# Attention in a fused attention pair: fp32 for a fourth of the first image's keys, earlier first scores, and two changes of order

## The chip, the cores and the metric

The kernel runs on one core of a Trainium2 chip. The metric is the device time of one execution in microseconds. Before the change the median of three runs is 2675.47 us (2675.39 to 2676.53). In what follows PE is TensorE (matmuls), DVE is VectorE, ACT is ScalarE, POOL is GpSimd, and SP is the engine that issues most of the transfers.

## The reference, cut to what matters

Two layers stand one after the other. Each has a group norm, attention over the 1024 positions of an image, a projection and a residual addition. The first layer has 8 heads of 64 channels, and its q, k and v go through an 8-bit quantization whose scale is taken over all 8 images. The second has one head of 512 channels.

```python
# layer 0: x is (8, 512, 32, 32), T = 1024, 8 heads
h = group_norm(xf, gn_w, gn_b)
qkv = jnp.einsum('oc,bct->bot', qkv_w, h) + qkv_b[None, :, None]
q, k, v = jnp.split(qkv.reshape(b * NUM_HEADS, -1, T), 3, axis=1)
q = fake_quant(q); k = fake_quant(k); v = fake_quant(v)
w = jnp.einsum('bct,bcs->bts', q * scale, k * scale)
w = jax.nn.softmax(w.astype(jnp.float32), axis=-1).astype(q.dtype)
a = jnp.einsum('bts,bcs->bct', w, v)
x = xf + jnp.einsum('oc,bct->bot', proj_w, a) + proj_b[None, :, None]
# layer 1: one head of 512
t = group_norm(x).transpose
qk = jnp.einsum('bnd,bmd->bnm', q, k) * scale
out = jnp.einsum('bnm,bmd->bnd', jax.nn.softmax(qk, axis=-1), v)
x = x + out @ wp.T + bp
```

## The kernel before, in words

**Three stages.** The first (0 to about 612 us) makes q, k and v of all eight images and stores them in DRAM, since the quantization needs the extremes of all of them. The second (612 to about 773 us) runs image 0's attention, and beside it `fold`: the second layer's weights are multiplied with one another, in eight pieces of four fp32 matmuls (`fold`, four into `wa` and four into `wm`), followed by two weighings of biases (`wt_f`, `wc_f`). In the third, `layer1(b)` of image b fills PE while the attention of image b + 1 is laid in between.

**Attention (`attention`, L832).** A unit is one pair of heads, one half `hf` of 512 queries and one block `s` of 128 keys; an image has 4 pairs x 2 halves x 8 blocks = 64 units. `scores` (L844) makes the scores in a PSUM pair `st`, of which there are two (two matmuls, one per head of the pair), and ACT writes their exponentials to `pt` (fp32, four buffers). `split` (L867) turns `pt` into two fp16 parts: a cast to fp16 gives the first, and a subtraction on DVE, pt minus the first part, gives the second. The cast stands on POOL for s = 2 and 6, on DVE for s = 1 and 5 as long as the order is not planned, and on ACT otherwise. `over_keys` (L897) sums v over the keys with both parts (four matmuls of 64 output columns into `av`), `totals` (L913) sums ones over them (four matmuls of 32 columns into `sm`). After a half, `finish` copies `av` to `ao` and `sm` to `rs` on ACT; after the second half the row sums go through DRAM, are inverted, and `ao` is scaled.

**The order.** The generator yields after every four units. In each such advance the scores of units u + 6 and u + 7 come first, then the sums of u and u + 1, the scores of u + 8 and u + 9, and the sums of u + 2 and u + 3 (`dense`), or all four units' sums at once (not `dense`). During `fold` an `advance()` runs whenever `pos < (folded - F_FIRST) * A_IMAGE / F_FOLD`; with F_FIRST = 12 the first scores stand after the fourth piece. Two advances more (`LEAD`) follow image 0, on image 1's units, and then the order of DVE, ACT and PE is written out: `InOrder` gives each instruction a dependency on the one before, and `later` puts chores with a cost and a due time into a list from which `fill` takes them; `settle(name)` issues all chores of a name at once.

**Loads.** `load_pair` (L795) fetches q, k and v of a pair into `raw` buffers (two), and two DVE steps each (`quant`, `quant2`) quantize them. With two buffers, v's load waits until q's has been read.

**Layer 1.** `o_run` (L1277) makes the second layer's attention output in seven products (`seven`), whose sums of operands are made by DVE: p2 for the third product, p3 for the fourth, p4 later. At its first product it yields 1, which lets an advance of attention in, and only then settles p2. In `first` (L1486), the next image's projection yields -1 between its halves (a dense advance) and 1 after the second. Projection and scores share the PSUM pool `ps_s`.

Of the kernel before, what the change touches and what calls it, by code (L numbers as in the profile page):

```python
# [9 lines left out]
F32 = mybir.dt.float32  # L10
# [7 lines left out]
P = 128  # L18
B, C, HH, WW = 8, 512, 32, 32
T = HH * WW  # L20
# [33 lines left out]
def attn_pair_kernel(  # L54
# [12 lines left out]
    class InOrder:  # L67
# [71 lines left out]
        def settle(self, what):  # L139

            while True:
                i = next((i for i, c in enumerate(self.chores) if c[0] == what), None)
                if i is None:
                    return
                self.begin(i)
# [143 lines left out]
    with ExitStack() as fast:  # L289
# [4 lines left out]
        def av_bank(name):  # L294
            return ps_v.tile([P, 512], F32, tag="v", name=name)
# [480 lines left out]
        def inverse(sm, rows, at, scratch, nm):  # L776
# [13 lines left out]

            return rest

        ao = {}

        def load_pair(b, j):  # L795

            nm = f"{b}_{j}"
            raws = []

            def fetch(i, src):  # L800
                raw = raw_p.tile([P, T], F32, tag="raw", name=f"raw_{nm}_{i}")
                nc.sync.dma_start(
                    raw if i < 2 else raw.rearrange("p (t d) -> p t d", t=NT), src
                )
                raws.append(raw)

            fetch(0, q_d[b][j])
            fetch(1, k_d[b][j])
            qt = qkp.tile([P, T], BF, tag="q", name=f"q_{nm}")
            kt = qkp.tile([P, T], BF, tag="k", name=f"k_{nm}")  # L810
            vt = qkp.tile([P, NT, P], F16, tag="v", name=f"v_{nm}")
            todo = (qt, kt, vt.rearrange("p t d -> p (t d)"))

            def quants(i):
                for step in (quant, quant2):
                    dve.later(
                        "qk" if i < 2 else "qv", 0.7, lambda step=step: step(raws[i], todo[i], i),
                        pe.t + 12.0, 45.0,
                    )

            def fetch_v():
                fetch(2, v_d[b][:, :, bass.ts(j, P)])
                quants(2)

            quants(0)
            quants(1)
            dve.later("qk", 0.0, fetch_v)
            return qt, kt, vt

        settle = dve.settle  # L830

        def attention():  # L832
# [8 lines left out]
            pts, parts, avs, sms, rss, ready = {}, {}, {}, {}, {}, {}  # L841
            st_free, at_hand = [0.0, 0.0], set()

            def scores(u):  # L844
                b, j, hf, s = units[u]
                if hf == 0 and s == 0:
                    settle("qk")
                nm = f"{b}_{j}_{hf}"
                qt, kt, _ = pairs[b, j]
                st = pair_ps(f"st_{nm}_{s}")  # L850
                awaits(st_free[-2])
                for i, r in enumerate(HALF):
                    mm(
                        st[:, i, :], lhsT=kt[r, bass.ts(s, P)],
                        rhs=qt[r, bass.ts(hf, 512)], start=True, stop=True,
                    )
                if u >= 4:
                    need(u - 4)
                pt = ptp.tile([P, 2, 512], F32, tag="p", name=f"pt_{nm}_{s}")
                there = act.do(  # L860
                    1.12, lambda: act.activation(pt, st, AF.Exp, scale=esc),
                    max(pe.t + 0.25, ready.get(u - 4, 0.0) + 0.1),
                )
                st_free.append(there)
                pts[u] = pt, there

            def split(u):  # L867

                b, j, hf, s = units[u]
                pt, there = pts.pop(u)  # L870
                two = partp.tile([P, 2, 2, 512], F16, tag="two", name=f"two_{b}_{j}_{hf}_{s}")
                parts[u] = two

                def rest():
                    dve.tensor_tensor(two[:, 1], pt, two[:, 0], ALU.subtract)
                    ready[u] = dve.t

                def cast(copy=act.copy):
                    at_hand.add(u)
                    copy(two[:, 0], pt)  # L880
                    done_at = act.t if copy == act.copy else there + 1.5
                    dve.later("sum", elements(1024), rest, done_at + 0.1, 9.0)

                if s % 4 == 2:
                    cast(nc.gpsimd.tensor_copy)
                elif not InOrder.planned and s % 4 == 1:
                    cast(dve.tensor_copy)
                else:
                    act.later("cast", 1.02, cast, there, 7.0)
# [7 lines left out]
            def over_keys(us):  # L897
                need(us[-1])
                awaits(ready[us[-1]])
                pe.t += 0.12  # L900
                for u in us:
                    b, j, hf, s = units[u]
                    if s == 0:
                        avs[b, j, hf] = av_bank(f"av_{b}_{j}_{hf}")
                    for w in range(2):
                        for i, r in enumerate(HALF):
                            mm(
                                avs[b, j, hf][r, :], lhsT=pairs[b, j][2][:, s, r],
                                rhs=parts[u][:, w, i, :], start=(s == 0 and w == 0),
                                stop=(s == NT - 1 and w == 1),  # L910
                            )

            def totals(us):  # L913
                pe.t += 0.12
                for u in us:
                    b, j, hf, s = units[u]
                    if s == 0:
                        sms[b, j, hf] = av_bank(f"sm_{b}_{j}_{hf}")
                    two = parts.pop(u)
                    for n in range(4):  # L920
                        mm(
                            sms[b, j, hf][n * QUAD : (n + 1) * QUAD, :], lhsT=ones16,
                            rhs=two[:, n // 2, n % 2, :], start=(s == 0), stop=(s == NT - 1),
                        )

            def finish(b, j, hf):

# [43 lines left out]
            for u in range(0, len(units), 4):  # L971
                b, j, hf, s = units[u]
                if hf == 0 and s == 0:
                    n = b * PAIRS + j + 1
                    if n < B * PAIRS:
                        pairs[divmod(n, PAIRS)] = load_pair(*divmod(n, PAIRS))
                    settle("qv")

                def two(what, v):
                    if v < len(units):
                        what(v)
                        what(v + 1)

                pe.t += 0.12
                two(scores, u + 6)
                if dense:
                    over_keys((u, u + 1))  # L990
                    totals((u, u + 1))
                    two(split, u + 6)
                    two(scores, u + 8)
                    over_keys((u + 2, u + 3))
                    totals((u + 2, u + 3))
                else:
                    over_keys(range(u, u + 4))
                    totals(range(u, u + 4))
                    two(split, u + 6)
                    two(scores, u + 8)  # L1000
                if s == NT - 4:
                    finish(b, j, hf)
                two(split, u + 8)
                pe.t += 0.15
                last = (j, hf, s) == (PAIRS - 1, NH - 1, NT - 4)
                yield 6.0 + (hf == NH - 1 and s == NT - 4), b + last
# [270 lines left out]
        def o_run(b, hf, vt, vs, ps_, pts, acc, rx, between):  # L1277
# [50 lines left out]
            for step in seven(  # L1328
# [2 lines left out]
                lambda n, ps: act.do(0.59, lambda: act.copy(u[n], ps)), whole, add,  # L1331
            ):
                if step == 1:
                    yield 1
                elif step == 2:
                    settle("p2")
                elif step == 3:
                    settle("p3")
                if step == 2 + (hf == NH - 1 and not final):
# [47 lines left out]
        def layer1(b, steps):  # L1387
# [36 lines left out]
            for hf in range(NH):  # L1424
# [39 lines left out]
                def third(p12=p12, p22=p22):  # L1464
# [2 lines left out]

                dve.later(
                    "p2", elements(1024), lambda t1=t1, t2=t2, p22=p22: tt(t2, p22, t1, ALU.subtract),
                    dve.t, 5.0,  # L1470
                )
                dve.later("p3", elements(1024), third, act.t, 9.0)
                dve.later(
# [10 lines left out]
                if b + 1 < B and last:  # L1484

                    def first():  # L1486
                        nonlocal ahead
                        yield -1
                        yield from project(b + 1, score_bank)
                        yield 1  # L1490
                        ahead = norm1(b + 1, score_bank)
                        next(ahead)

                    def more():
                        next(ahead)
                        yield from ()

                    between = [first, more, more]
# [93 lines left out]
        att = attention()  # L1592
        A_IMAGE = PAIRS * (NH * NT * 1.5 + 1.0)
        F_FOLD = 4.0 * 8 + 2.0
        F_FIRST = 12.0
        pos, done = 0.0, 0
        dense = True

        def advance():
            nonlocal pos, done  # L1600
# [26 lines left out]
            e.t = pe.t  # L1627
        InOrder.planned = True
        for n in others():
            dense = n < 0  # L1630
            advance()


# [362 lines left out]
```

## Time and profile before

| what | us |
|---|---|
| median of three runs | 2675.47 |
| the profiled execution | 2674.34 |
| its span, first to last instruction | 2672.5 |
| PE busy in it | 2582.6 (97%) |
| DVE, ACT, POOL busy | 1909.5, 1263.1, 204.1 |
| PE waiting between 612 and 775 us for exponentials (`pt`) | 30.7 |
| first scores of image 0 | 626.83 |
| first projection matmul of image 0 | 773.58 |

The busy times are sums over the whole span, and the stages differ: in the first and third PE hardly waits, in the second it does. So a row is read by its stage. A row of waits names the engine and what it would have gone on with, then the engine whose work ended last among what it waited for. Rows in order of time give start, length, engine, operation, output and inputs; an instruction's length can overlap with the next one's by a tenth of a microsecond, so that the spacing of a run of equal ones is shorter than the length of one.

### The profile page before, as it was taken

The page shows a single profiled execution, that of the slowest core. Times are in us where ns is not written, and L with a number is a line of the kernel's source. Part 1 is how long each engine was busy: PE and PEld are TensorE (multiplying, and loading weights), DVE is VectorE, ACT ScalarE, POOL GpSimd, SP SyncE. Part 2 cuts the span into 40 slices and gives each one's busy share as a digit, 9 for nine tenths or more (in the row PEclk, how much of TensorE's full clock was granted, in tenths as well). Part 3 has the DMA queues.
Part 4 walks back from the last instruction along what each step waited for, and adds up shares of the span by engine and source line. Part 5 has one row for each costly group of instructions (what it writes and reads, how often), then busy time and mean ns, then how long its engine had stood idle before and what let it go on. Part 6 is the DMA issues. An engine that isn't in the chain of part 4 may idle for free.

```text
span 2672.5 us, 33466 instructions
## 1 busy us (share of the span) xinstructions
PE 2582.6 (97%) x13150; PEld 1663.0 (62%) x13150; DVE 1909.5 (71%) x2755; ACT 1263.1 (47%) x1588; POOL 204.1 (8%) x157
## 2 busy tenths in 40 slices
PE   8999999998788999999999999999999999999998
PEld 4655555553225775776577567757765775677687
DVE  7866666558987767886777677768867776876544
ACT  0111111115866674666566556646664665564121
POOL 0000000001220000000100010001001000100000
PEclk9999999999899999999999999999999999999999
DMA  5233232134321132223212321322132123212211
GB/s 201 112 125 126 110 119 94 73 124 150 121 67 45 57 108 83 84 68 102 96 60 76 111 88 56 107 84 84 58 109 99 60 76 107 86 42 73 106 36 37
DMA packets 146888, 241.97 MB, mean 91 GB/s; under 512 B 26528, under 2 KB 92064, under 8 KB 145184
## 3 DMA queue, kind: packets, MB, share of 16 engines
q1 hardware_dynamic: 115872, 181.50, 20.3%
q10 hardware_dynamic: 30848, 58.23, 6.4%
q8 instruction: 105, 1.72, 0.3%
q14 instruction: 63, 0.52, 0.1%
HBM read 152.86 MB, written 86.28 MB: 89 GB/s over the span
## 4 chain that ended last, share of the span: by engine, by line
PE 80%; DVE 8%; issue 7%; ACT 2%; DMA 1%; POOL 1%; ACTq 0%; SPq 0%; DVEq 0%; POOLq 0%
PE s L201 15%; PE o L201 14%; PE qkps L201 10%; PE pj L201 8%; PE av L201 7%; PE v2ps L201 7%; PE g L201 6%; PE vps L201 5%; PE st L201 4%; PE sm L201 4%; DVE two L86 2%; ACT pt L86 1%; DVE sums L86 1%; DVE x L86 1%; DVE h L86 1%
## 5 line engine op out<-in xcount | busy, mean ns | idle before, releaser
L86 DVE TENSOR_TENSOR two<-pt,two 128x1024 f16<-128x1024 f32 x512 | 618.4, 1225 | 164.7 <-POOL two L880 131.1
L86 ACT ACTIVATE pt<-st,esc 128x1024 f32<-128x1024 f32 x512 | 543.8, 1114 | 371.4 <-PE st L201 349.9
L86 ACT CAST two<-pt 128x1024 f16<-128x1024 f32 x364 | 369.3, 1054 | 9.6 <-issue 5.6
L880 POOL CAST two<-pt 128x1024 f16<-128x1024 f32 x128 | 179.5, 1402 | 1578.7 <-PE sm L201 1352.0
L86 ACT ACTIVATE u<-qkps,qkb 128x512 f32<-128x512 f32 x90 | 61.8, 687 | 500.8 <-PE qkps L201 500.8
L201 PE MATMUL av<-two,v 128*64 128x512 f16 x2048 | 254.3, 386 | 0.6
L201 PE MATMUL s<-g,h 128*128 128x256 f32 x1024 | 234.1, 381 | 0.0
L201 PE MATMUL pj<-ao,wp 128*128 128x512 f32 x512 | 223.9, 595 | 1.1 <-DVE ao L86 1.1
L201 PEld LDWEIGHTS s<-g,h 128*128 128x128 f32 x1024 | 193.0, 190 | 31.7 <-issue 4.3
L201 PE MATMUL st<-q,k 64*128 64x512 bf16 x1024 | 166.6, 387 | 40.0 <-ACT pt L86 33.5
L201 PEld LDWEIGHTS <-v 128*64 128x64 f16 x2048 | 103.8, 110 | 132.7 <-issue 61.4
L201 PE MATMUL s<-g,sums 128*128 128x256 f32 x768 | 178.4, 381 | 0.2 <-DVE p L86 0.2
L201 PE MATMUL o<-p,v 128*128 128x256 f32 x768 | 175.2, 382 | 0.0
L201 PEld LDWEIGHTS pj<-ao,wp 128*128 128x128 f32 x512 | 96.1, 190 | 122.6 <-issue 112.6
L201 PE MATMUL qkps<-sums,wa 128*128 128x512 f32 x360 | 164.9, 592 | 0.1
L201 PEld LDWEIGHTS o<-p,v 128*128 128x128 f32 x768 | 144.4, 190 | 25.6 <-issue 6.9
L201 PEld LDWEIGHTS s<-g,sums 128*128 128x128 f32 x768 | 144.8, 190 | 24.1 <-issue 4.5
L201 PE MATMUL sm<-two,ones 128*32 128x512 f16 x2048 | 141.8, 386 | 1.9 <-ACT rs L86 1.9
L201 PE MATMUL qkps<-x,wqkv 128*128 128x512 f32 x304 | 140.8, 602 | 1.3 <-DVE x L86 1.3
L201 PEld LDWEIGHTS <-k 64*128 64x128 bf16 x1024 | 36.4, 94 | 163.9 <-issue 161.9
L201 PE MATMUL o<-g,vsum 128*128 128x256 f32 x512 | 123.7, 397 | 11.5 <-DVE g L86 11.5
L201 PE MATMUL g<-h,wa 128*128 128x256 f32 x512 | 120.6, 384 | 1.7 <-DVE h L86 1.7
(193 smaller groups left out, 3524.9 us busy)
## 6 DMA issues: line engine op xcount, KB each, us to landing
rs<-rs_d SPq DMA_DIRECT2D x80, 256.0 KB
x<-in_x_dram SPq DMA_DIRECT2D x32, 512.0 KB
raw<-q_d SPq DMA_DIRECT2D x32, 512.0 KB
raw<-k_d SPq DMA_DIRECT2D x32, 512.0 KB
v_d<-v SPq DMA_DIRECT2D x32, 512.0 KB
raw<-v_d SPq DMA_DIRECT2D x32, 512.0 KB
x_d<-h SPq DMA_DIRECT2D x64, 256.0 KB
x<-x_d ACTq DMA_DIRECT2D x64, 256.0 KB
```

The lines of the kernel that those rows point to most:

```text
L86: ins = self.latest = op(*args, **kw).ins
L201: ins = nc.tensor.matmul(ps, lhsT=lhsT, rhs=rhs, **kw).ins
L880: copy(two[:, 0], pt)
```

## The change

Image 0's units with s = 3 and s = 7 (`plain`) are no longer split: their exponentials go into a buffer `aside` of three slots, and `over_keys` and `totals` take them as fp32, with an fp32 copy of v's blocks 3 and 7 (`vfs`, made by a third DVE step `whole`) and the fp32 ones. The cast on DVE stays for s = 5 alone. The first v has a buffer of its own (`raw_first`, one of the `ao` buffers), and its load is issued at once. F_FIRST goes from 12 to 4. In `o_run`, p2 is settled before the yield of the first product, and its chore's due time is set to be first. After the second half of a projection, `first` yields 2, for which the advance has another order (`late`): sums of u and u + 1, scores of u + 6, totals, sums and totals of u + 2 and u + 3, then splits and scores of u + 8.

```diff
+        def plain(b, s):
+            return b == 0 and s % 4 == 3
...
             def fetch(i, src):
-                raw = raw_p.tile([P, T], F32, tag="raw", name=f"raw_{nm}_{i}")
+                if (b, j, i) == (0, 0, 2):
+                    raw = aop.tile([P, NH, 512], F32, tag="ao", name="raw_first").rearrange(
+                        "p h n -> p (h n)"
+                    )
+                else:
+                    raw = raw_p.tile([P, T], F32, tag="raw", name=f"raw_{nm}_{i}")
...
+            def whole(raw, _, i):
+                quant2(raw.rearrange("p (t d) -> p t d", t=NT)[:, 3::4, :], vfs[j], i)
...
+            if b == 0:
+                vfs[j] = xp.tile([P, 2, 256], F32, tag="x", name=f"vf_{nm}")[:, :, 0:P]
...
-                for step in (quant, quant2):
+                for step in (quant, quant2, *([whole] if i == 2 and b == 0 else [])):
...
             def fetch_v():
+                if len(raws) == 2:
+                    fetch(2, v_d[b][:, :, bass.ts(j, P)])
+                quants(2)
+
+            if (b, j) == (0, 0):
                 fetch(2, v_d[b][:, :, bass.ts(j, P)])
-                quants(2)
-
...
+            aside = l2p.tile([P, 3, NT // 2, 256], F32, tag="vsum", name="aside")
...
-                pt = ptp.tile([P, 2, 512], F32, tag="p", name=f"pt_{nm}_{s}")
+                if plain(b, s):
+                    pt = aside[:, u // 4 % 3].rearrange("p (i k) n -> p i (k n)", i=2)
+                else:
+                    pt = ptp.tile([P, 2, 512], F32, tag="p", name=f"pt_{nm}_{s}")
...
+                if plain(b, s):
+                    parts[u], ready[u] = pt, there
+                    return
...
-                elif not InOrder.planned and s % 4 == 1:
+                elif not InOrder.planned and s == 5:
...
+                    if plain(b, s):
+                        for i, r in enumerate(HALF):
+                            mm(
+                                avs[b, j, hf][r, :], lhsT=vfs[j][:, s // 4, r],
+                                rhs=parts[u][:, i, :], start=False, stop=(s == NT - 1),
+                            )
+                        continue
...
+                    for n in range(2 if plain(b, s) else 4):
+                        row = sms[b, j, hf][n * QUAD : (n + 1) * QUAD, :]
+                        if plain(b, s):
+                            mm(row, lhsT=ones[:, 0:QUAD], rhs=two[:, n, :], start=False,
+                               stop=(s == NT - 1))
+                        else:
+                            mm(row, lhsT=ones16, rhs=two[:, n // 2, n % 2, :], start=(s == 0),
+                               stop=(s == NT - 1 - (b == 0 and n > 1)))
...
-                two(scores, u + 6)
-                if dense:
+                if not late:
+                    two(scores, u + 6)
+                if late:
+                    over_keys((u, u + 1))
+                    two(scores, u + 6)
+                    totals((u, u + 1))
+                    over_keys((u + 2, u + 3))
+                    totals((u + 2, u + 3))
+                    two(split, u + 6)
+                    two(scores, u + 8)
+                elif dense:
...
                 if step == 1:
+                    settle("p2")
                     yield 1
-                elif step == 2:
-                    settle("p2")
...
                     "p2", elements(1024), lambda t1=t1, t2=t2, p22=p22: tt(t2, p22, t1, ALU.subtract),
-                    dve.t, 5.0,
+                    0.0, 0.5,
...
                         yield from project(b + 1, score_bank)
-                        yield 1
+                        yield 2
...
-        F_FIRST = 12.0
+        F_FIRST = 4.0
...
-            dense = n < 0
+            dense, late = n < 0, n == 2
```

More of the change, by code (lines that the diff above doesn't have):

```diff
@@ L791, in inverse @@
             return rest
+        vfs = {}
+        def plain(b, s):
+            return b == 0 and s % 4 == 3
         ao = {}
@@ L919, in totals @@
                     two = parts.pop(u)
[L920 to L924, printed above, removed]
+                    for n in range(2 if plain(b, s) else 4):
[6 more added lines that the diff above has]
+                               stop=(s == NT - 1 - (b == 0 and n > 1)))
             def finish(b, j, hf):
@@ L1594, in attn_pair_kernel @@
         F_FOLD = 4.0 * 8 + 2.0
-        F_FIRST = 12.0
+        F_FIRST = 4.0
         pos, done = 0.0, 0
         dense = True
+        late = False
         def advance():
```

## The prediction

> **What bounds the kernel now.** I read the page's chain first, then TensorE's waits over the whole span, then the same waits by stretch, then the order of time at the two places where they pile up. All times are of the one profiled execution. The chain's shares by engine, and the waits (total, times, longest):
>
> ```profile
> PE 80%; DVE 8%; issue 7%; ACT 2%; DMA 1%; POOL 1%; ACTq 0%; SPq 0%; DVEq 0%; POOLq 0%
> ```
>
> ```profile
> PE st L201 <- ACT pt L86: 33.5, 50, 1.6
> PE o L201 <- DVE g L86: 11.5, 6, 1.9
> ...
> PE st L201 <- DVE h L86: 6.2, 12, 0.5
> ```
>
> TensorE sets the end, and is busy 97%, so a gain has to come out of its few waits or its busy time. These three waits hold 51 us. By stretch, 30.7 of the 33.5 us for `pt` fall between 612 and 775 us, where image 0's attention runs with only the folding beside it; the other two recur in the later images: six times 1.9 us before an `o` product, and twelve times 0.52 us before scores that follow a half of the projection.
>
> ```profile
> 720.00:760.00 40.00, 29.11 (x226) 8.80 (x223) 39.06 (x39) 35.99 (x39) 12.99 (x6) 0.87 0.25 80
> ```
>
> This is a row of the busy times by stretch: length, then PE, its weight loads, DVE, ACT, POOL, then granted clock and DMA. In image 0's attention DVE (39.06 of 40) and ACT (35.99) are full and PE is not. How this stage starts:
>
> ```profile
> 621.81 6.53 DMA raw<-v_d
> ```
>
> ```profile
> 633.09 6.07 PE L201 MATMUL fold<-wn_v 128*128 128x512 f32 x8
> ...
> 645.47 3.70 PE L201 MATMUL fold<-wn_v 128*128 128x512 f32 x8
> ```
>
> The first line is of the chain followed back from 660 us: it runs over the load of the first v, which waits for q's raw buffer. The other two are of the order of time: the folding piece at 633 took 6.07 us, the same piece at 645 3.70.
>
> ```profile
> 991.79 0.25 DVE L86 RECIPROCAL rcs<-rcs 128x16 f32<-128x16 f32 x1
> ...
> 994.36 1.23 DVE L86 TENSOR_TENSOR two<-pt,two 128x1024 f16<-128x1024 f32 x1 [2.31 <-ACT two L86]
> ...
> 1002.79 1.22 DVE L86 TENSOR_TENSOR g<-p,g 128x1024 f32<-128x1024 f32 x1
> ...
> 1004.06 3.72 PE L201 MATMUL o<-g,vsum 128*128 128x256 f32 x16 [1.91 <-DVE g L86]
> ```
>
> The sum `g<-p,g` (p2 in the code) has had its data since 991.78, when the exponential of p ends, but stands on DVE behind a burst of attention's subtractions, while DVE idles 2.31 us at 992.
>
> [...] the four 32-wide `wt_f` products (8 records, two of 0.43 us for each matmul) take 1.03 to 1.06 us together. [...] The piece of 6.07 us agrees; it follows 6 us of sparse scores with a granted clock of 0.61 in 630 to 635. [...] The casts on POOL agree: 1.04 us alone, up to 3.55 beside DVE.
>
> **Part A, image 0 in fp32 for a fourth of the keys.** For 16 of 64 units the cast and the subtraction go, and s = 1 is cast on ACT where DVE did it. Spacings from back-to-back rows: exponential 1.01, ACT cast 0.95, copy 0.47, DVE subtraction 1.13, DVE cast 0.60, quantizing step 0.68.
> Per half (8 units), before: ACT 8 x 1.01 + 4 x 0.95 + 2 x 0.47 = 12.8; DVE 8 x 1.13 + 2 x 0.60 + 3 x 0.68 + 0.75 = 13.05. Copies of `ao` mark the ends of the halves: 654.80, 670.35, 685.61, 700.58, 717.87, 732.94, 747.72, 761.34, 775.06; the two clean ones take 13.62 and 13.72, 0.6 over DVE's sum.
> After: ACT 8.08 + 3 x 0.95 + 0.94 = 11.9; DVE 6 x 1.13 + 0.60 + 3 x 0.68 + 0.25 + 0.75 = 10.4. ACT becomes the bound. PE: a split unit costs 0.25 (scores) + 0.49 + 0.27; in a plain one av is 0.86 and sm 0.86, if the two halves run together. No row shows a 64-wide fp32 pair; from below 0.86 by `wt_f`, from above 1.72 in series. I take 0.86: 6 x 1.01 + 2 x 1.97 = 10.0 per half. In order: counted from the start of the first exponential of a group, PE has given out that group's second scores at 0.5, does 0.49 + 0.86 + 0.27 + 0.86 = 2.5 us of sums with a plain unit, and the next scores by 3.45, where ACT is busy until 2 x 1.01 + 2 x 0.95 = 3.9: it fits, by 0.45. Clean half: 11.9 + 0.5 = 12.4.
> With a folding piece (3.44 + a copy of 0.58 on ACT, both ahead of the next exponential) that cover is gone: scores come at 3.0 + 3.45 + 0.5, and ACT waits about 3.2. Half: 11.9 + 3.2 + 0.4 = 15.5, no better than now (15.55, 15.26, 14.97).
>
> **Part B, earlier start.** F_FIRST = 4 puts the first scores after two pieces (PE 619.8, q and k quantized at 619.85) instead of four (626.83). v's own buffer waits for a PE read that ends at 610, so its load is issued about 610.2, ahead of q_d and k_d stores on SP, which are due at 611.0 anyway; against 6.53 us for the same load later it lands about 616, before its place on DVE at 617.8. If late, q and k stand behind it: up to 1 us. The fp32 copy of v waits for those stores, about 622.5 to 624.5; behind it stand the z sums and the first subtraction, due about 627, needed by exponential 5 at 627.8. Counted at nothing, up to 1.4 if not. Pair 1's q and k, behind the 1 MB of `wp` on SP but no longer behind v, land by about 630, before their place. The buffers taken (one `ao` of five, `vsum`, two of `x`) are next wanted after 764, when they are free: nothing.
> The two pieces come back into the attention, so it meets six, not four. Going through the order by hand (exponential 0 at 620.6, 1.01 each, casts 0.95, the next piece at half clock like the one at 633, so 6.1), the first half's `ao` copy is at 647.5 instead of 654.80: 7.3.
> Then four halves with a piece 4 x 15.5, one with the weighing of biases 16.3 (its stall of 3.5 on ACT by the same chain, and 0.5 for the last `wc_f`), two clean 2 x 12.4, and image 1's first half, which is split throughout and has now five ACT casts: 14.3. Sum 117.4 against 120.3: 2.9. Stage: 7.3 + 2.9 = 10.2 us, from 4 to 15.
>
> **Part C, the sum ahead of the burst.** p2 moves into the idle 2.31 us at 992, takes 1.2, delays nothing. The `o` product then starts at 1002.15. Late next: the third operand. DVE after the kept_u addition: three acc at 0.69 from 1002.79, then the 1.13 us sum, done at 1006.07; PE needs it at 1005.80 + 0.36 = 1006.16. It fits by 0.1. 6 x 1.91 = 11.5, at least 9. For the other half of each image (seen at 907.87) DVE now waits 1.7 us for the exponential with three subtractions behind it; the one that is needed, for PE's fourth pair of av at about 910.9, ends at 908.65. Nothing.
>
> **Part D, late order.** After the second half of a projection the av of two units (0.98 us) now stand before the scores, and cover DVE's eviction (0.52). The scores, and so the exponentials, start about 1 us later, with PE filled till 1052.6 when the eighth needs its slot at 1051.75. I take 0.4 x 6 = 2.4 us, from 0 to 3.1. The first half of each projection keeps its wait.
>
> **Sum.** 10.2 + 11.5 + 2.4 = 24.1. The profiled execution took 2674.34 (span 2672.5 and 1.84 around it), 1.1 below the median of the runs, 2675.47: 2650.2 on it, 2651.3 on the median. I say 2651.
>
> **Rivals.**
> The stage gives nothing, the waits do: the 64-wide pairs run in series (0.86 more for av, so 1.3 per half over the cover, about 10 in all). For: no such row; against: `wt_f`. 2661.
> The next wait takes p2's place: one subtraction more ahead of the third operand costs 6 x 1.1 = 6.6, 2658. For: cover of 0.1 only; against: the order in the program puts none there.
> The pieces cost ACT less, as now, where a half with one is about 1.5 over a clean one: five times about 1.7 less, 2642. For: those halves; against: PE has 2 us more in each now.
> Slower: in the plain units each 64- or 32-wide fp32 product runs alone with its two weight loads (0.11 each) in the open: 4 x 1.08 = 4.3 us per unit for 1.72, 2.6 more; 16 x 2.6 less the cover of 16 x 0.25 is 38, so 2689. It decides from 24.1 / 16 + 0.25, 1.8 us per unit. Against: loads of f16 weights lie under the products in this stage, and `wt_f`.
> That the change does not do what it says: the built order of instructions shows the plain products, the early scores and the moved sum in place.
>
> **How the numbers follow.** Forecast 0.57, stage nothing 0.15, next wait 0.08, cheap pieces 0.12, slower 0.05, and 0.03 for a loss of the gain to several of the bounds. Bounds of A and B (4 to 15), C (9 to 11.5), D (0 to 3.1) give 13 to 30, 2645 to 2662; with the rivals 2642 to 2663. A measurement tells 0.2% (5 us) from no change: faster 0.92, within 0.03, slower 0.05.
>
> **What would show it.** A: ACT over 95% busy in 640 to 750 us, DVE near 85%; `av<-pt` pairs spaced 0.86. B: first scores near 620, first `ao` copy near 647.5, halves of 12.4 and 15.5; projection starting near 763. C: no wait of `o` for `g`. D: six waits of 0.5 left, not twelve. It is wrong if halves with pieces exceed 17, or if `o` waits for p instead of g.

## The result, and the profile after

The changed kernel takes 2643.61 us (median of four runs, 2642.59 to 2645.55), the kernel before 2675.55: a ratio of 0.9881, 95% interval 0.9864 to 0.9898, so 31.9 us less. The forecast was 2651 in a range of 2642 to 2663, some 24 us less. The gain is there and the range holds it, but 7.8 us of it (31.9 less 24.1) were not in the sum. The profiled execution after took 2642.96 us with a span of 2641.2.

Where it came from can be read off points that both traces have. The times are starts from the order of time; the last column is how far the changed kernel is ahead by then.

| point | before | after | ahead |
|---|---|---|---|
| first folding matmul | 612.90 | 612.67 | 0.23 |
| first scores of image 0 | 626.83 | 619.74 | 7.09 |
| first copy of `ao` | 654.80 | 646.78 | 8.02 |
| ninth copy of `ao` (image 1's first half) | 775.06 | 762.77 | 12.29 |
| second half of image 0's projection | 793.35 | 780.29 | 13.06 |
| third step of the first `g` products | 838.30 | 827.39 | 10.91 |
| projection of image 7 | 2477.23 | 2446.88 | 30.35 |
| end of the span | 2672.5 | 2641.2 | 31.3 |

So the stage gave 12 to 13 us by these two traces, some 2 were lost right behind it, and the six images with an attention beside them gave 19.4, where parts C and D of the forecast had 13.9. About 1 us of the stage's part is within what executions differ by: from the first folding matmul to the ninth copy of `ao` the trace of before has 162.2 us, three other traces with the same stage (the sum alone, the filled wait and the late order alone, below) 161.2 to 161.4, the changed kernel 150.1. First the page's chain of work that ended last, by engine, and then TensorE's waits over the whole span (total us, times, longest), both of the changed kernel:

```profile
PE 83%; DVE 8%; ACT 3%; issue 2%; DMA 2%; POOL 1%; SPq 0%; ACTq 0%; DVEq 0%; POOLq 0%
```

```profile
PE st L201 <- ACT pt L86: 11.9, 17, 2.5
...
PE st L201 <- ACT aside L86: 6.1, 14, 0.6
...
PE st L201 <- DVE h L86: 3.1, 6, 0.5
...
PE o L201 <- DVE p L86: 1.0, 6, 0.2
```

The wait of `o` for `g` is gone; what is late next is the third operand, p, by 0.16 us a time. Six of the twelve waits for `h` are left. The waits of scores for exponentials (`pt` and `aside` together) fell from 33.5 to 18.0.

Busy times by stretch in the changed kernel (length, then PE, weight loads, DVE, ACT, POOL, granted clock, DMA):

```profile
720.00:760.00 40.00, 33.52 (x262) 10.22 (x260) 34.04 (x36) 39.18 (x44) 10.91 (x7) 1.00 0.36 117
640.00:680.00 40.00, 37.94 (x238) 11.49 (x240) 32.64 (x36) 32.11 (x37) 7.01 (x5) 1.00 0.24 78
```

Two different limits lie side by side. From 640, where every half has a piece of folding, PE is busy 37.94 of 40 us and ACT only 32.11; from 720, without pieces, ACT is full and PE has room. DVE, which was full before (39.06), is full in neither. The granted clock differs in this stage too: its mean is 0.93 from 612 to 775 us before, and 0.98 from 612 to 765 after; how much of the stage's gain comes with that, no run separates. What a half with a piece and a plain unit looks like on PE, in order of time:

```profile
675.76 0.62 PE L201 MATMUL av<-two,v 128*64 128x512 f16 x4
676.22 1.02 PE L201 MATMUL av<-aside,vf 128*64 128x512 f32 x4
677.17 0.40 PE L201 MATMUL sm<-two,ones 128*32 128x512 f16 x4
677.40 1.02 PE L201 MATMUL sm<-aside,ones 128*32 128x512 f32 x4
```

A plain unit's two fp32 products are 4 records within 1.02 us, and the next group starts 0.95 after them: the two run side by side, and their weight loads (0.36 and 0.33 us from first to last) lie under other work: PE is busy without a break from 675.76 to 678.95.

And the moved sum, on DVE in the changed kernel:

```profile
981.07 1.16 DVE L86 TENSOR_TENSOR g<-p,g 128x1024 f32<-128x1024 f32 x1
984.27 1.22 DVE L86 TENSOR_TENSOR two<-pt,two 128x1024 f16<-128x1024 f32 x1 [2.04 <-ACT two L86]
```

It stands ahead of the burst, in what was idle time, ten microseconds before the product that needs it (991.07).

What the forecast missed shows in the trace of before, once one looks behind the wait. PE in order of time, kernel before, the same product after the same wait in two neighbouring images:

```profile
1248.71 5.41 PE L201 MATMUL o<-g,vsum 128*128 128x256 f32 x16 [1.92 <-DVE g L86]
...
1495.08 3.72 PE L201 MATMUL o<-g,vsum 128*128 128x256 f32 x16 [1.92 <-DVE g L86]
```

and the busy times of those stretches (the clock is the third figure from the end):

```profile
1248.00:1252.00 4.00, 3.29 (x8) 2.63 (x9) 3.93 (x6) 0.75 (x1) 0.00 (x0) 0.61 0.06 19
1495.00:1499.00 4.00, 3.92 (x24) 3.12 (x24) 3.93 (x6) 0.23 (x2) 0.00 (x0) 1.00 0.00 0
```

After every second of these waits (1248.71, 1739.74, 2230.77) the granted clock falls, and the product takes 1.69 us longer. That is 5.1 us in three places, and none of it is counted as a wait, since PE is busy. So far this is only read from traces; the first two experiments test it.

### The profile page after: what moved, and what is told of

It reads as the page before. It is cut to its first block, busy times and chain, and to the rows that moved or that the text cites. A ratio compares the mean times of both kernels' runs of the same rounds, so it can differ in the third digit from the quotient of the medians.

```text
span 2641.2 us, 33393 instructions
## 1 busy us (share of the span) xinstructions
PE 2585.6 (98%) x13150; PEld 1657.2 (63%) x13150; DVE 1880.1 (71%) x2733; ACT 1256.9 (48%) x1582; POOL 195.7 (7%) x157
## 4 chain that ended last, share of the span: by engine, by line
PE 83%; DVE 8%; ACT 3%; issue 2%; DMA 2%; POOL 1%; SPq 0%; ACTq 0%; DVEq 0%; POOLq 0%
PE s L201 15%; PE qkps L201 13%; PE o L201 12%; PE pj L201 8%; PE av L201 7%; PE v2ps L201 7%; PE vps L201 6%; PE g L201 5%; PE st L201 4%; PE sm L201 4%; ACT pt L86 2%; DVE two L86 1%; DVE sums L86 1%; DVE x L86 1%; DMA out_dram<-x 1%
## 5 line engine op out<-in xcount | busy, mean ns | idle before, releaser
L86 DVE TENSOR_TENSOR two<-pt,two 128x1024 f16<-128x1024 f32 x496 | 596.7, 1219 | 143.6 <-POOL two L909 114.1
L86 ACT ACTIVATE pt<-st,esc 128x1024 f32<-128x1024 f32 x496 | 527.0, 1116 | 355.3 <-PE st L201 335.5
L86 ACT CAST two<-pt 128x1024 f16<-128x1024 f32 x358 | 362.3, 1056 | 8.4 <-issue 5.8
L909 POOL CAST two<-pt 128x1024 f16<-128x1024 f32 x128 | 171.0, 1336 | 1553.6 <-PE sm L201 1028.1
L201 PE MATMUL av<-two,v 128*64 128x512 f16 x1984 | 246.0, 383 | 0.0
L201 PEld LDWEIGHTS s<-g,h 128*128 128x128 f32 x1024 | 192.8, 190 | 31.9 <-issue 4.3
L201 PEld LDWEIGHTS <-v 128*64 128x64 f16 x1984 | 98.1, 109 | 133.5 <-issue 65.6
L201 PE MATMUL v2ps<-wm,h 128*128 128x256 f32 x512 | 119.9, 383 | 0.7
```

What stands on the lines that cost most here:

```text
L86: ins = self.latest = op(*args, **kw).ins
L201: ins = nc.tensor.matmul(ps, lhsT=lhsT, rhs=rhs, **kw).ins
```

## The experiments

All ratios below are to runs of the kernel before on the same chip, beside the run in question; its median was 2677.3 to 2678.7 us there. Intervals are 95%. Differences in us are the ratio times that time.

**The moved sum alone.**

```diff
                 if step == 1:
+                    settle("p2")
                     yield 1
-                elif step == 2:
-                    settle("p2")
...
-                    dve.t, 5.0,
+                    0.0, 0.5,
```

> Kernel before with part C alone (the p2 sum settled ahead of the yield). Theory: the six waits of 1.91 us go (11.5), and with them the fall of TensorE's clock that follows every second one (the o product after it took 5.41 us in place of 3.72 at 1248.71, 1739.74 and 2230.77; 3 x 1.69 = 5.1): 2675.5 - 16.6 = 2659, and no o product of 5.4 us is left. Rival 1: the clock falls for another reason, at the same places: 2675.5 - 11.5 = 2664, with three products of 5.4 us still there. Rival 2: the surplus over the forecast comes from the parts together: 2664 or more, with the clock at 1.00.

Measured: 2659.98 us, ratio 0.9933 (0.9919 to 0.9946), 17.9 us less (14.5 to 21.7). The 11.5 us of the waits lie outside of this, the 16.6 with the clock inside. In its trace no `o` product of 5.4 us is left, and the wait of `o` for p is 0.9 us in six times. Rival 1 falls: with the wait, its aftermath goes. Rival 2 falls as well, since the sum alone gives at least 14.5.

**The wait kept, TensorE given something to do in it.** This leaves the late sum where it was and lets only the idle time shrink.

```diff
                 awaits(free[(i + turn) % 2])
+                if i == 2 and nm.startswith("o2_") and nm.endswith("_1") and nm[3] in "012345":
+                    at = pe.t
+                    left, right = pairs[1]
+                    for k in range(2):
+                        mm(
+                            y[:, 0, :], lhsT=left[:, k, 0:P], rhs=right[:, k, :],
+                            start=True, stop=True, skip_group_check=True,
+                        )
+                    pe.t = at
                 product(n, ps, start)
```

> Kernel before, with two matmuls of 256 columns of no use (0.86 us) put ahead of the third product of the second half in images 0 to 5, into a bank that the product after it overwrites: they can run from the eviction at about 1002.85, so PE idles about 0.7 and 0.3 us in place of 1.9, and p2 comes as late as before. Theory (an unbroken wait of 1.9 us lets the clock fall in every second image): no o product of 5.4 us is left, 2675.5 - 5.1 = 2670.4. Rival 1 (the clock falls for another reason): 2675.5. Rival 2 (1 us of idle time in pieces is enough): products of 5.4 us remain, 2674 to 2676.

Measured: 2671.99 us, ratio 0.9977 (0.9968 to 0.9986), 6.2 us less (3.8 to 8.6). PE in order of time in this kernel, at the place that the kernel before shows at 1248.71:

```profile
1250.45 1.13 PE L201 MATMUL o<-p,v 128*128 128x256 f32 x4 [0.78 <-DVE kept_u L86]
1251.58 3.72 PE L201 MATMUL o<-g,vsum 128*128 128x256 f32 x16
```

0.78 of waiting and 1.13 of useless work are the same 1.91 us, so the product starts as late as before (5.63 us after the start of the product ahead of it, in both kernels). Only the clock differs, and the product takes 3.72 us, here and in the five other images. The kernel is faster for six pairs of matmuls that compute nothing. Both rivals fall. This shows that the idle time, not the place or the program, brings the slower product, and that its price is about 5 us here. The granted clock in single places varies from run to run elsewhere too (0.79 with the order alone from 824 to 832 us, 1.00 in the kernel before), so the 6.2 isn't a finer measure of it than the traces' 5.1.

**The late order alone.**

```diff
-                two(scores, u + 6)
+                if not late:
+                    two(scores, u + 6)
+                if late:
+                    over_keys((u, u + 1))
+                    two(scores, u + 6)
...
-                        yield 1
+                        yield 2
```

> Kernel before with part D alone (the late order after the second half of a projection). Theory: six of the twelve waits of 0.52 us for h are covered, six of about 0.45 net as between the traces (1281.44 to 1299.96 was 18.52 us, after it 18.06): 2675.5 - 2.7 = 2672.8. Rival (the exponentials then start later, and PE waits for them): 2675.5.

Measured: ratio 0.9995 (0.9987 to 1.0003), 1.3 us less, between 3.5 less and 0.8 more: by the time alone this decides nothing between 2.7 and none. The waits do:

```profile
PE o L201 <- DVE g L86: 11.5, 6, 1.9
...
PE st L201 <- DVE h L86: 3.1, 6, 0.5
```

Six waits for `h` are gone, and from the second half of image 1's projection to the `o` product behind it the trace has 18.07 us (1035.68 to 1053.75), before 18.53. So the step works, 0.46 us in each image. The time is too coarse for that: the 13 executions of this kernel lie between 2671.6 and 2681.3 us, and the trace is of one of the two fastest (2671.96). In it the clock is at 0.79 from 824 to 832, where the kernel before has 1.00; 0.21 of 8 us is 1.7 us at most, an estimate; so single falls of the clock differ from one execution to the next by about as much as this step gives.

**The stage alone** (parts A and B). Against the changed kernel, the sum and the order are undone:

```diff
                 if step == 1:
-                    settle("p2")
                     yield 1
+                elif step == 2:
+                    settle("p2")
...
-                        yield 2
+                        yield 1
```

> Kernel before with parts A and B alone (fp32 units, earlier first scores, own buffer of the first v). Theory: the stage gives 12.3 us by the last ao copy and 1.3 by the wait of the first projection for ao that is gone, less up to 1.7 where the clock falls at about 817: 2675.5 - 13.6 = 2661.9, up to 2663.6. Rival (the later images gained nothing from the sum and the order but what 11.5 and 2.4 say, and the stage gave the rest of 31.9): 2657.5.

Measured: 2662.69 us, ratio 0.9943 (0.993 to 0.9957), 15.3 us less (11.5 to 18.8). The interval takes in both. The trace tells them apart: from the second half of image 0's projection to the projection of image 7 it has 1684.24 us (783.28 to 2467.52), the kernel before 1683.88. The later images have nothing from the stage, so the rival falls.

**Part A alone and part B alone.** A is the stage's kernel with F_FIRST at 12 and v in the old buffer, B the kernel before with these two edits and nothing of `plain`:

```diff
-        F_FIRST = 12.0
+        F_FIRST = 4.0
...
+                if (b, j, i) == (0, 0, 2):
+                    raw = aop.tile([P, NH, 512], F32, tag="ao", name="raw_first").rearrange(
```

> Kernel before with part A alone (fp32 units for s = 3 and 7, first scores still behind four pieces of folding). Theory from the halves of the two traces: a half with a piece of folding takes 15.25 us in both kernels, but one without 12.5 to 13.0 in place of 13.6 to 15.1; with only four pieces in the attention five halves are free of them, so A alone gives 8 to 10 us, and B adds some 4 to that. Rival (as the forecast split it): the start gives 7.3 and belongs to B, the halves give 2.9: A alone 3 us.

> Kernel before with part B alone (first scores behind two pieces of folding, own buffer of the first v). Theory from the run with A alone: the start is 7 us earlier, but two more halves have a piece and then take 15.25 us in place of 13.7 to 14.8, so that B alone gives 4 to 5 us. Rival (as the forecast split it): 7.3 us, and A and B together then give less than their sum.

Measured: A alone 0.9969 (0.9958 to 0.9979), 8.3 us less (5.6 to 11.2); B alone 0.9983 (0.9976 to 0.999), 4.6 us less (2.7 to 6.4). Both rivals fall, and the sum of the two, 12.9, lies within the 15.3 (11.5 to 18.8) of A and B together. The forecast divided the stage by time, 7.3 us in the start and 2.9 in the halves, and had no figure for either edit alone. Taken as the shares of B and A these two would be wrong: most of the gain is A's. In the trace with B alone the first `ao` copy comes at 647.20, 7.6 us ahead of the kernel before, and the ninth at 770.53, only 4.5 ahead (counted from the first folding matmul, which comes 0.9 us later in this trace, 8.5 and 5.4): two pieces more stand in the attention, and the halves with folding take 15.3 to 18.4 us.

**The changed kernel itself, beside the next two:**

> The changed kernel as it is, as a measure for the other runs beside it: 32 us less than the kernel before.

Measured: 2645.99 us, 0.9885 (0.9869 to 0.99), 30.8 us less.

**The late order after both halves of a projection.**

```diff
                 if hf + 1 < NH:
-                    yield -1
+                    yield 2
```

> The changed kernel with the late order after the first half of each projection too. Theory: the other six waits of 0.52 us for h are covered as the first six were: 2.7 us less than the changed kernel. Rival (after the first half the exponentials have no lead to give away, and PE waits for pt or the sums instead): no less, or up to 3 us more.

Measured: 2647.64 us, 0.9888 (0.9873 to 0.9904), no less than the changed kernel. The waits of this kernel:

```profile
PE st L201 <- ACT pt L86: 11.7, 16, 2.5
...
PE pj L201 <- ACT pt L86: 6.0, 6, 1.0
```

No wait for `h` is left, and in its place the second half of the projection waits 0.99 us for an exponential, six times: projection and scores share their PSUM pool, and with the scores later, the bank comes free later. From one half of the projection to the next the trace has 19.13 us (1003.85 to 1022.98), the changed kernel 18.76. The rival holds.

**The folding spread in twos, and more evenly still.** The changed kernel's fold loop is replaced by `slip(n)`, which issues n of the folding's matmuls (`fold` yields after each of them instead of after each piece):

```diff
+                if u < 4:
+                    slip(2)
                 yield 9.0 if u else 0.0, 0
...
                     over_keys((u + 2, u + 3))
                     totals((u + 2, u + 3))
+                    if b == 0:
+                        slip(2)
...
-        for w in fold():
-            folded += w
-            while pos < (folded - F_FIRST) * A_IMAGE / F_FOLD:
-                advance()
+        slip(8)
```

> The changed kernel with the folding's 24 later matmuls put in two at a time: two behind each of the first two groups of scores, then two after the last sums of each advance of image 0, in place of a piece of four after every second advance; the copy of a finished piece follows with the next two. Theory: in a half with a piece ACT waits 2.8 us for the piece, which stands ahead of the scores, while PE is busy 9.3 tenths; spread, ACT has casts to do meanwhile, and the half takes what PE has to do, about 13.5 us in place of 15.25: 6 x 1.7 = 10 us less than the changed kernel, from 5 to 12. Rival (the half is bound by PE's own order, and two matmuls delay the scores as four do, twice as often): no less, or more.

Measured: 2641.51 us, 0.9862 (0.9847 to 0.9877). The interval overlaps that of the changed kernel beside it. In the traces, from the first scores to the first projection matmul, it is 139.17 us (622.49 to 761.66) against 142.40 (622.42 to 764.82): 3.2 us less, not the 10 of my estimate. All of that is in the start, where two matmuls of folding fill PE's waits behind each of the first groups of scores: to the first `ao` copy 22.73 us in place of 27.25. The five halves with folding or weighing aren't shorter in sum (15.95, 14.17, 15.03, 15.03 and 16.94 us, 77.1 together; 15.25 to 15.34, 76.4 together, in the changed kernel). What ACT waits for between 640 and 720 us in the changed kernel, and then in the spread one:

```profile
ACT wm L86 <- PE fold L201: 11.2, 4, 2.8
ACT wa L86 <- PE fold L201: 2.8, 1, 2.8
```

```profile
ACT pt L86 <- PE st L201: 5.7, 4, 1.4
ACT wm L86 <- PE fold L201: 3.2, 4, 1.0
```

ACT waits less for the folding and more for the scores, because it is PE that is full: 38.06 of 40 us between 680 and 720. I had taken 10.0 + 3.4 us of PE work for such a half; at 37.94 of 40 us busy, a half of 15.25 us in the changed kernel holds some 14.5. The median of the spread version is the lowest of all, but as the intervals overlap, it is not shown to be faster than the changed kernel.

The even order, against the spread kernel; here the loads of `wp` and of the second layer's x stand before the first and the second weighing:

```diff
                     if b == 0:
-                        slip(2)
+                        slip(2 - u // 4 % 2)
```

> As the spread kernel, but with two and one of the folding's matmuls by turns, so that they reach to the last half of image 0 (and wp and the second layer's x loaded before the weighings). Theory (the halves with folding are bound by PE, at 95% busy, the last three by ACT, with PE idle for 7.3 us of 40): the folding moves out of the full halves into PE's idle time there, 4 to 7 us less than the spread kernel in the stage. Rival (what waits in the last halves is ACT's exponentials, and the matmuls there delay scores): no less.

Measured: 2646.06 us, 0.9886 (0.9871 to 0.9901), and from first scores to projection 143.47 us (620.21 to 763.68): nothing gained. Five halves do come down to between 13.8 and 14.2 us. But the sparser PE also meets short waits, and the clock falls. Busy times by stretch in this kernel:

```profile
676.00:678.00 2.00, 1.37 (x16) 0.49 (x16) 1.97 (x3) 1.04 (x2) 0.00 (x0) 1.00 0.00 0
678.00:680.00 2.00, 0.99 (x10) 0.34 (x8) 2.00 (x2) 2.00 (x3) 1.04 (x1) 0.99 0.00 0
680.00:682.00 2.00, 2.00 (x9) 0.58 (x8) 2.00 (x4) 2.00 (x3) 0.00 (x0) 0.50 0.00 0
682.00:684.00 2.00, 2.00 (x10) 0.33 (x8) 1.20 (x2) 1.46 (x2) 0.00 (x0) 0.66 0.50 147
```

After 1.64 us of waits in three pieces between 677 and 680 (0.63, 0.40, 0.61), the clock is 0.50. That half took 17.33 us, and another with a clock of 0.50 at 746, which also holds weighings, 17.88. The clock is not all of it: in either half it is at 0.50 for 3.4 us, which costs at most half of that, 1.7 (an estimate), and these halves are over 3 us longer than the five. Against the spread kernel, the five halves after the first `ao` copy take 2.1 us less together, and the last three, into which the folding was moved, 5.6 more (45.79 in place of 40.16). That fits the rival; what part of it the clock has isn't shown.

## Why the prediction was right, and which term was mis-sized

**Part C.** The mechanism was right: the sum moved into DVE's idle time, and six waits went; only the third operand came later for it. The term "6 x 1.91 = 11.5, at least 9" was mis-sized: it priced a wait by its length. It measured 11.5 net of waits (about 2.04 less in each image up to the `o` product, 0.13 of it given back behind) and 5.1 of slower products, 16.6 in all. The bounds "9 to 11.5" left out the upper side. The trace of before would have told it: three of the six products after the wait are 5.41 us long. In that trace the granted clock is 0.50 for 3.41 us in each of the three places (1248.87 to 1252.28, 1740.39 to 1743.80, 2231.91 to 2235.32). Half of 3.41 is 1.7 us, an estimate of what it costs, and the trace has 1.69 (5.41 less 3.72). So gaps of 1.9 us cost the clock in three of six cases. At the folding piece of 6.07 us, where the prediction gives a mean clock of 0.61, PE was idle for 2.63 of the 3.41 us before 631.06, and from there to 637.88 the clock was 0.50.

**The third operand.** I had it in time by 0.1 us; it is 0.16 late. Six times this is the 1.0 us of `o` for p. By the letter this is one of the prediction's signs of being wrong, `o` waiting for p instead of g; in size it is 1.0 us against the 11.5 that went, and the rival in which it takes the place of p2 (6.6 us) did not happen.

**Part D.** 2.4 us forecast; 0.46 in each of six images measured from trace to trace, 2.8.

**Parts A and B.** 10.2 forecast, 12.3 by the last `ao` copy. By terms: the first `ao` copy was put at 647.5 and came at 646.78; halves with a piece at 15.5, measured 15.25 to 15.26; the half with weighings at 16.3, measured 15.34; the clean ones at 12.4, measured 12.47 and 13.01; image 1's half at 14.3, measured 14.15. Taking 0.86 us for the 64-wide fp32 pair was nearly right (0.95 measured), and so both rivals that rested on its price, the pairs in series and the open weight loads, fell. The rival with cheap pieces named 2642 us, which is about what was measured, but not for its reason: a half with a piece took 15.25 us, 2.2 to 2.8 over a clean one, and not 1.5. Two things need correcting though the sum came out, which is luck in part. ACT was to be over 95% busy from 640 to 750: it is so only without pieces (39.18 of 40), with pieces it is 32.11, and PE is the limit. I had counted the half by ACT's stall and not seen that the stall was PE's full schedule. And the 7.3 us until the first `ao` copy come with B alone too (7.6 in its trace), but they don't last: B alone keeps 4.6 in the end, while A alone gives 8.3.

**Not in the sum.** The first projection no longer waits 1.06 us for `ao`, so 0.77 us more are gained by its second half; right behind it 2.15 are lost, 0.45 by a longer wait for `h` and the rest where the clock falls, in the changed kernel after a wait of 3.69 us for `g`'s operands:

```profile
816.00:820.00 4.00, 4.00 (x13) 3.21 (x12) 2.51 (x4) 0.84 (x2) 0.00 (x0) 0.59 0.41 110
```

The kernel before has nearly the same wait (3.68) and kept its clock. The traces show which of such waits is hit. In each of the twelve, all changes of the granted clock lie on a grid of 3.413 us (to within 0.006 us), and each execution has its grid elsewhere. In the changed kernel one step of the grid, 812.47 to 815.88, holds 2.26 us of the wait, and the clock is at half in the next. In the kernel before, an edge at 825.62 cuts the wait into 1.98 and 1.71 us, and the clock stays. First two steps of the changed kernel, then two of the kernel before:

```profile
812.47:815.88 3.41, 1.16 (x6) 1.06 (x6) 3.41 (x6) 2.22 (x3) 0.00 (x0) 1.00 0.13 20
815.88:819.29 3.41, 3.41 (x10) 2.70 (x9) 2.63 (x4) 0.84 (x2) 0.00 (x0) 0.50 0.51 138
```

```profile
822.21:825.62 3.41, 1.43 (x7) 0.93 (x5) 3.38 (x7) 3.16 (x5) 0.00 (x0) 1.00 0.00 0
825.62:829.03 3.41, 1.70 (x8) 1.55 (x9) 3.41 (x6) 1.68 (x2) 0.00 (x0) 1.00 0.31 95
```

Eleven traces have this wait at 3.7 us. In the eight where a step holds at least 2.14 us of it, the clock falls; in the three where none holds more than 1.98 (before, the stage alone, the changed kernel's second trace), it doesn't. The waits of 1.92 us for `g` follow the same pattern. Five traces have thirty of them: of the 17 that lie whole in one step, 16 are followed by a fall (the exception ends at 1986.09 in the kernel before), and of the 13 that an edge cuts, none. So the 5.1 us of the kernel before are three hits out of six in this one execution, and another execution can have more or fewer.

The last 0.95 us lie behind the last product, where the end of the span varies by as much from trace to trace, though none of the kernels changes anything there (20.2 to 21.6 us from the start of the last `o<-g,vsum` product).

## What to carry to other kernels

Price a stall of TensorE by its length and by what the work behind it then takes: compare the durations of the same product after the wait in several repetitions, and if some are longer, the wait costs more than the table of waits says. How many are longer differs from one execution to the next (of the six products behind 1.92 us, three in four traces, four in a fifth), so one trace gives no fixed price. Where one stage holds two kinds of stretches, count each engine's work for each kind; here removing DVE's limit showed PE as the limit beside the folding and ACT without it. And a wait that is covered on one side of a shared buffer can come back on the other: the same late order gave 0.46 us after one half and cost 0.4 after the other.

## What the runs showed of the hardware

The granted clock changed only on a grid of 3.413 us. An unbroken idle time of 1.92 us on TensorE was followed by a fall of it in 16 of 30 places: in three of six in the kernel before, the run with the stage alone, the one with part A alone and the one with the order alone, and in four of six with part B alone. It was so in 16 of the 17 places where this time lay whole in one step of the grid, and in none of the 13 where an edge cut it. With 0.78 us of it left idle and 1.13 filled it was so in none of six. Waits of 0.63, 0.40 and 0.61 us within one step (676.55 to 679.96) were enough once. Two matmuls that do nothing, put into a wait that can't be removed, paid for themselves: 6.2 us less (3.8 to 8.6) for six such pairs.
